# First layer of a graph network: who issues the edge-attribute loads

## The chip, the cores and the metric

The kernel runs on one core of a Trainium2 chip. The metric is the device time of one execution in microseconds (us); smaller is better. Before the change three runs gave 4244.64, 4257.71 and 4271.31 us, a median of 4257.71 us.

A core has five engines with an instruction stream each: TensorE (PE; its weight loads are PEld), VectorE (DVE), ScalarE (ACT), GpSimd (POOL) and SyncE (SP). SyncE computes nothing. DMA transfers are carried out by 16 DMA engines. An engine that issues a transfer spends an instruction on it; the transfer then runs by itself, and a semaphore tells of its landing. An engine executes its instructions in order: if one waits for a semaphore, all behind it wait too.

## The reference

Four layers are added to a residual stream `x` of 6250 nodes with 256 features; each begins with a layer norm. The change concerns the first one, a message-passing layer over 106,250 edges sorted by destination:

```
h   = relu(concat(xn[src], edge_attr) @ W1 + b1)     # one row per edge
agg = segment_sum(h, dst) / max(count, 1)            # mean over the edges of a node
x   = x + relu(concat(xn, agg) @ W2 + b2)
```

The attributes are 106,250 rows of 256 f32, about 109 MB, and each row is used once. The other three layers (graph attention with four experts, a second graph layer, and a mixture of small networks) are not touched.

## The kernel before

**Work of the first layer.** The product with W1 is split. `xn @ W1[:256] + b1` is computed once per node in an opening loop (L1534) and stored to a table in DRAM, `y_dram` (L1554, issued by SyncE). After that, each edge needs its attribute row times the other half of W1, plus the gathered row `y_dram[src]`.

Nodes are taken in 49 windows of 128. The edges of a window make a fixed stretch of tiles of 128 edges, cut into three groups of six tiles; so there are 147 groups, numbered `q`. For each group:

- `load_attr` (L1494) takes one of three `ea` buffers and lists the loads that fill it: the six tiles come in two or three runs of tiles that lie together, and each run is cut into four loads by column block (`for c in (0, 2, 1, 3)`). A group with three runs of two tiles has twelve loads of 64 KB, a group with two runs of three tiles has eight of 96 KB. Two groups of each window have three runs and one has two: 32 loads a window, 1568 in all.
- `issue` (L1515) starts the listed loads from the front of the list, each on the engine that its entry names.
- `turn` (L1610, `V.transpose` at L1613) transposes `ea` into `et` on VectorE. It is the only reader of `ea`, so its end frees the buffer.
- `hidden` (L1618) multiplies `et` with `w1b` on TensorE, two tiles at a call (the matmuls are recorded at L1170, in the helper `mm`).
- `load_sources` (L1603) gathers `y_dram[src]` by six indirect DMAs from GpSimd (L1184), into a ring of four buffers.
- `join` (L1628) adds both on VectorE (L1631) and takes the relu on ScalarE (L1632).
- `add_up` (L1635, L1650) sums the rows into their nodes on TensorE.

When a window's three groups are summed, `end_of` (L1656) finishes its nodes in small steps over the next groups: ScalarE scales and copies (L1663, L1165, L1685, L1691, L1702 to L1704), TensorE transposes (L1164) and multiplies (L1170), VectorE adds. Beside this, in the same loop, VectorE sorts the edges of the second layer, and `windows` prepares the edge indices of later windows (two small loads by SyncE for each window, L1202).

**Order.** The loop at L1741 writes the order out by hand, and `Ordered.pin` keeps it on every engine. In round `q` the loads for the next groups are handed out at three places (L1753, L1762, L1768), up to four from the list (`LOT = 4`) at each. Loads for group `q + 4` are listed after `turn(q + 1)`, whose end frees their buffer. In the opening loop, from the fifth block of nodes on, the loads of the first three groups are issued in one go (L1568, L1569), between the node work.

**Who issues.** The entry's engine is `SY if c < 2 or i == 2 else SC`. Of a group with three runs SyncE issues eight loads and ScalarE four, of a group with two runs each issues four; in total SyncE 980 and ScalarE 588. Each load's address depends on the window's first edge, a value that `start_of` (L1093) reads from SBUF into a register of both engines (TENSOR_LOAD at L1094).

**Semaphores of the loads.** In the trace the loads of both engines use eight semaphores in turn. A load waits until the load eight before it, whichever engine issued that one, has landed; the first load into a buffer also waits for VectorE's transpose.

Of the kernel before, what the change touches and what calls it, by code (L numbers as in the profile page):

```python
# [918 lines left out]
def kernel(ctx: ExitStack, tc: tile.TileContext, a: dict, out: bass.AP):  # L919
# [73 lines left out]
    V, SC, TE, GP, SY = nc.vector, nc.scalar, nc.tensor, nc.gpsimd, nc.sync  # L993
# [7 lines left out]
    with ExitStack() as fast:  # L1001
# [91 lines left out]
        def start_of(w, *also):  # L1093
            return nc.values_load(  # L1094
                start[0:1, w : w + 1], engines=(mybir.EngineType.SP, *also), min_val=0,
                max_val=E1 - WE, skip_runtime_bounds_check_because="it is clamped to that",
            )
# [350 lines left out]
        with ExitStack() as layer:  # L1448
# [45 lines left out]
            def load_attr(q):  # L1494

                w, g = groups1[q]
                parts = []
                ea = wea.tile([P, G1 * 4, 2 * Q], F32, name="ea")
                r = start_of(w, mybir.EngineType.Activation)
                rows = a["edge_attr_256"][bass.ds(r, WE), :]  # L1500
                at = 0
                for i, (first, n) in enumerate(RUNS[g]):
                    part = rows[first * P : (first + n) * P, :]
                    for c in (0, 2, 1, 3):
                        parts.append((
                            SY if c < 2 or i == 2 else SC,
                            ea[c * Q : (c + 1) * Q, at : at + 4 * n, :],
                            part[:, 2 * c * Q : 2 * (c + 1) * Q].rearrange(
                                "(m p) d -> p m d", p=Q
                            ),  # L1510
                        ))
                    at += 4 * n
                return ea, parts
# [8 lines left out]
            with (  # L1522
# [11 lines left out]
                for t0, t1 in parts0:  # L1534
# [32 lines left out]
                    if b >= 4:  # L1567
                        ahead[b - 4], parts = load_attr(b - 4)  # L1568
                        issue(parts, len(parts))  # L1569
# [3 lines left out]
            with (  # L1573
# [167 lines left out]
                for q in range(NQ1 + 2):  # L1741
                    if 0 < q <= NQ1:
                        join(q - 1)
                    if q < NQ1:
                        hidden(q, 0)
                    steps(keys or sort)
                    if q >= 2:
                        add_up(q - 2)
                        if (q - 2) % NG == NG - 1:
                            work.append(end_of((q - 2) // NG))  # L1750
                    if 3 <= q + 2 < NQ1:
                        load_sources(q + 2)
                    issue(parts, LOT)  # L1753
                    if q + 1 < NQ1:
                        turn(q + 1)
                    for n in range(q + 2, min(q + 5, NQ1)):
                        if n not in ahead:
                            ahead[n], more = load_attr(n)
                            parts += more
                    if q < NQ1:  # L1760
                        hidden(q, 2)
                    issue(parts, LOT)  # L1762
                    steps(keys or (sort if q % 4 else []))
                    if q < NQ1:
                        equals[q] = equal(wk, *groups1[q])
                        hidden(q, 4)
                    steps(slow)
                    issue(parts, LOT)  # L1768
                    ordered.pin()
# [1084 lines left out]
```

## Time and profile before

| | us |
|---|---|
| median of three runs | 4257.71 |
| the profiled execution, its own time | 4246.74 |
| its span on the core | 4244.9 |
| first layer's group loop, from about 100 to 1510 us of the span | 1410 |
| TensorE busy in that stretch | 1185.76 |
| VectorE, GpSimd, ScalarE busy in that stretch | 908.97, 854.48, 321.89 |

Some 2 us of the profiled execution lie outside its span. The page gives the busy time of each engine, the span in 40 slices, the DMA queues (q1 is filled by SyncE, q10 by ScalarE, q0 by GpSimd's gathers), and groups of instructions. Instructions that issue a DMA or wait for a semaphore are not counted as busy; they are marked with a q behind the engine (SPq, ACTq). The view of waits has one line for each pair of a waiting instruction and what ended its wait, with total, number of times and the longest; "issue" is idle time that ended with nothing that the profile shows, and "remote" is a semaphore whose sender it can't name.

### The profile page before, as it was taken

The page shows a single profiled execution, that of the slowest core. Times are in us where ns is not written, and L with a number is a line of the kernel's source. Part 1 is how long each engine was busy: PE and PEld are TensorE (multiplying, and loading weights), DVE is VectorE, ACT ScalarE, POOL GpSimd, SP SyncE. Part 2 cuts the span into 40 slices and gives each one's busy share as a digit, 9 for nine tenths or more (in the row PEclk, how much of TensorE's full clock was granted, in tenths as well). Part 3 has the DMA queues.
Part 4 walks back from the last instruction along what each step waited for, and adds up shares of the span by engine and source line. Part 5 has one row for each costly group of instructions (what it writes and reads, how often), then busy time and mean ns, then how long its engine had stood idle before and what let it go on. Part 6 is the DMA issues. An engine that isn't in the chain of part 4 may idle for free.

```text
span 4244.9 us, 59987 instructions
## 1 busy us (share of the span) xinstructions
PE 3208.8 (76%) x18517; PEld 2451.9 (58%) x18517; DVE 2192.9 (52%) x6516; ACT 1188.6 (28%) x2200; POOL 2256.7 (53%) x2720
## 2 busy tenths in 40 slices
PE   6788888888888767777787777794347777767787
PEld 5566666666666555566666665672235555555556
DVE  6666667665666535546464544674223333434344
ACT  4122222222222223334444443572002111111133
POOL 1655666566666543445454445424566666665551
PEclk8899999999999988889998988895567767667687
DMA  5666777667676632223232332343111111111110
GB/s 176 153 160 156 165 169 166 161 160 169 156 171 162 147 84 69 65 64 104 73 101 75 81 87 67 95 108 90 42 47 50 51 50 51 50 49 52 46 48 19
DMA packets 704935, 423.34 MB, mean 100 GB/s; under 512 B 538699, under 2 KB 647303, under 8 KB 704604
## 3 DMA queue, kind: packets, MB, share of 16 engines
q1 hardware_dynamic: 422972, 201.12, 17.9%
q0 software_dynamic: 88512, 171.58, 17.0%
q10 hardware_dynamic: 193120, 46.69, 5.1%
q8 instruction: 150, 2.46, 0.2%
q14 instruction: 181, 1.48, 0.1%
HBM read 382.75 MB, written 42.50 MB: 100 GB/s over the span
## 4 chain that ended last, share of the span: by engine, by line
PE 40%; another core or an unknown queue 18%; issue 9%; DVE 8%; ACT 3%; DMA 1%; SPq 1%; POOL 0%; ACTq 0%; DVEq 0%; POOLq 0%
PE ph L1170 17%; PE py L1170 10%; PE pe L2714 5%; PE pt L1170 3%; PE pe L1650 2%; PE po L2032 1%; DVE et L1613 1%; DVE E L2010 1%; DVE eq L2691 1%; PE pa L1955 1%; ACT L1833 1%; PE pt L1164 1%; DMA rb<-low_dram 0%; SPq L1518 0%
## 5 line engine op out<-in xcount | busy, mean ns | idle before, releaser
L1184 POOL DMA_INDIRECT h<-y_dram,src x882 | 857.3, 972 | 639.0 <-issue 336.6
L1184 POOL DMA_INDIRECT hg<-hp_dram,src x831 | 784.2, 944 | 486.3 <-issue 224.7
L1184 POOL DMA_INDIRECT sg<-gat_dram,src x612 | 595.3, 973 | 722.9 <-DVE pay L1992 312.2
L1170 PE MATMUL ph<-w1b,et 128*128 128x256 f32 x3528 | 882.5, 397 | 82.7 <-issue 67.2
L1170 PEld LDWEIGHTS ph<-w1b,et 128*128 128x128 f32 x3528 | 673.6, 197 | 273.2 <-issue 181.9
L1170 PE MATMUL py<-w,hh 128*128 128x256 f32 x1568 | 449.8, 425 | 107.6 <-issue 52.1
L2714 PEld LDWEIGHTS pe<-eq,hg 128*128 128x128 f32 x2036 | 380.0, 259 | 224.8 <-issue 161.6
L2714 PE MATMUL pe<-eq,hg 128*128 128x96 f32 (+15 forms) x2036 | 390.2, 339 | 122.2 <-issue 76.6
L1170 PE MATMUL ph<-b_all,w 128*128 128x256 f32 (+1 forms) x1600 | 460.3, 427 | 13.8 <-issue 12.5
L2691 DVE TENSOR_SCALAR eq<-px,dst,ew 128x96 f32<-128x96 f32 x831 | 262.0, 369 | 324.4 <-remote 148.3
L1631 DVE TENSOR_TENSOR h<-ph,h 128x1536 f32<-128x1536 f32 x147 | 258.1, 1756 | 323.0 <-PE pe L1650 109.8
L1170 PEld LDWEIGHTS py<-w,hh 128*128 128x128 f32 x1568 | 303.4, 208 | 170.8 <-issue 67.8
L1632 ACT ACTIVATE h<-h 128x1536 f32<-128x1536 f32 x147 | 218.3, 1485 | 587.6 <-DVE h L1631 176.9
L1170 PEld LDWEIGHTS ph<-b_all,w 128*128 128x128 f32 x1600 | 317.2, 214 | 59.4 <-issue 19.8
L2010 DVE TENSOR_SCALAR E<-nodes,bits 128x256 bf16<-128x256 bf16 (+5 forms) x612 | 187.0, 339 | 174.9 <-remote 78.3
L1613 DVE STREAM_TRANSPOSE et<-ea 128x1536 f32<-128x1536 f32 x147 | 260.7, 1774 | 14.6 <-issue 8.5
L1833 ACT ACTIVATE hh<-ph,b 128x256 f32<-128x256 f32 (+1 forms) x400 | 166.0, 465 | 293.4 <-remote 137.1
L1650 PE MATMUL pe<-h,eq 128*32 128x257 f32 x2496 | 202.6, 410 | 13.5 <-issue 12.0
L1170 PE MATMUL py<-ew,g 65*128 65x256 f32 x392 | 141.8, 491 | 63.7 <-DVE x_all L2667 20.0
L1833 ACT ACT_TABLE_LOAD x102 | 130.9, 1283 | 91.5 <-remote 51.4
L2667 DVE SCALAR_TENSOR_TENSOR x_all<-py,gate,x_all 128x256 f32<-128x256 f32 x196 | 93.9, 479 | 110.7 <-remote 68.0
L2032 PE MATMUL po<-pays,E 128*128 128x61 bf16 x2116 | 117.2, 198 | 41.7 <-issue 33.1
(358 smaller groups left out, 3947.5 us busy)
## 6 DMA issues: line engine op xcount, KB each, us to landing
ea<-in_edge_attr_dram SPq DMA_DIRECT2D x784, 64.0 KB
ea<-in_edge_attr_dram ACTq DMA_DIRECT2D x392, 64.0 KB
w<-in_L_ffn_W_dram SPq DMA_DIRECT2D x48, 512.0 KB
y<-ys SPq DMA_DIRECT2D x96, 256.0 KB
rb<-low_dram SPq DMA_DIRECT2D x84, 256.0 KB
ea<-in_edge_attr_dram ACTq DMA_DIRECT2D x196, 96.0 KB
ea<-in_edge_attr_dram SPq DMA_DIRECT2D x196, 96.0 KB
h<-y_dram,src POOLq DMA_INDIRECT x882
```

The costliest lines, as they stand in the source:

```text
L1170: TE.matmul(dst, lhs(c), rhs(c), start=c == 0, stop=c == n - 1)
L1184: GP.indirect_dma_start(out=dst, out_offset=None, in_=table[0:NP, :], in_offset=IndirectOffsetOnAxis(ap=idx, axis=0), **more,)
L1613: V.transpose(et[q].rearrange("p c m k -> p m c k"), ahead.pop(q).rearrange("p m (c k) -> p m c k", c=2),)
L1631: V.tensor_add(h, ph.pop(q), h)
L1632: SC.activation(h, h, AF.Relu)
L1650: TE.matmul(sums[w][b * Q : (b + 1) * Q, :], some[:, (b - lo) * Q : (b - lo + 1) * Q], rows_of(q)[:, j, 0:WS], start=(g, b, j) in begin, s ...
L1833: SC.activation(hidden[u][:, f, :n, :], ph[:, f - f0, :n, :], AF.Gelu, bias=b1[:, e, f : f + 1],)
L2010: V.tensor_scalar(Es[g, j][:, 0:n, :].rearrange("p b k -> p (b k)"), nodes16[:, 0 : n * P], bits.bitcast(F32)[:, g * G + j : g * G + j + 1 ...
L2032: TE.matmul(pos[g][bank][:, to * HP : (to + 1) * HP], E[:, b - b0, :], pays[g % 2][:, j, :], start=bank not in begun, stop=bank not in lat ...
L2667: V.scalar_tensor_tensor(x_all[:, t, :], py[:, k, :], gate[:, t, e : e + 1], x_all[:, t, :], op0=OP.mult, op1=OP.add,)
L2691: V.tensor_scalar(equals[k][:, j, :], lanes[:, 0:NW], dst_of[:, t : t + 1], ew[:, t : t + 1], op0=OP.is_equal, op1=OP.mult,)
L2714: TE.matmul(sums[b][:, lo - t0 * P : hi - t0 * P], hg[:, j, :], eq[:, j, lo - n0 : hi - n0], start=False, stop=after >= (t0 + n) * P,)
```

## The change

Every load of the attributes is issued by SyncE. The list, its order, the sizes, the lots of four, the three places in a round, the buffers and what they wait for are the same.

```diff
                     for c in (0, 2, 1, 3):
                         parts.append((
-                            SY if c < 2 or i == 2 else SC,
+                            SY,
                             ea[c * Q : (c + 1) * Q, at : at + 4 * n, :],
```

In the built program ScalarE has 588 loads fewer and SyncE 588 more. ScalarE's register reads at L1094 are gone as well, since nothing there uses them. In the group loop the order of instructions on VectorE and GpSimd is the same as before; TensorE differs only in how a few matmuls and transposes of the opening loop alternate.

## The prediction

> **What bounds the kernel now.** I read the busy table by stretches first, because the change touches only the group loop, then the waits of TensorE, ScalarE and SyncE in its steady part, 200 to 1400 us, and last single moments. The table by stretches (columns after the length: PE, PEld, DVE, ACT, POOL busy, TensorE clock, DMA share, GB/s):
>
> ```profile
> core 0: us, PE busy (x) PEld busy (x) DVE busy (x) ACT busy (x) POOL busy (x), PEclk, DMA share, GB/s
> 200.00:1400.00 1200.00, 1015.16 (x5844) 744.37 (x5846) 786.70 (x1612) 277.75 (x460) 729.52 (x751) 0.95 0.69 162
> ```
>
> TensorE is busy 85% and nobody else over 66%: it is the bound, with 185 us of idle time in 1200. 124.5 groups pass in that time (147 in 1410 us), 9.6 us each. So the question is what the change does to TensorE's idle time. The waits of TensorE in the same window:
>
> ```profile
> PE ph L1170 <- issue: 60.1, 105, 1.7
> PE pt L1164 <- ACT a_dst L1704: 43.2, 13, 8.1
> PE pt L1170 <- issue: 21.6, 27, 4.8
> PE pt L1164 <- ACT o L1691: 20.9, 2, 13.0
> PE ph L1170 <- DVE et L1613: 5.8, 6, 2.0
> ```
>
> TensorE hardly ever waits for attributes (the transpose `et`: 5.8 us), and never for the relu. It waits for ScalarE in the steps of `end_of`, and for "issue". Of the two waits for `o` the longer is this moment, first on TensorE, then on ScalarE:
>
> ```profile
> 217.11 0.69 PE L1164 MATMUL pt<-ident,o 128*128 128x128 f32 x2 [13.03 <-ACT o L1691]
> ...
> 199.69 0.18 ACT L1685 ACTIVATE ln_rs<-ln_rs 128x1 f32<-128x1 f32 x1
> 214.81 1.52 ACTq L1518 DMA_DIRECT2D ea<-in_edge_attr_dram  x2
> 216.46 0.60 ACT L1691 ACTIVATE o<-x_all,off,ln_rs 128x256 f32<-128x256 f32 x1 [16.58 <-DMA ea<-in_edge_attr_dram]
> ```
>
> ScalarE stands from 199.9 to 214.8 before a load: its semaphore is still held by loads that SyncE issued, and the activation that TensorE needs is queued behind it. The views of ScalarE's and SyncE's waits, same window:
>
> ```profile
> ACT h L1632 <- DMA ea<-in_edge_attr_dram: 102.8, 23, 11.5
> ACT o L1691 <- DMA ea<-in_edge_attr_dram: 41.2, 3, 16.6
> ACT o L1663 <- DMA ea<-in_edge_attr_dram: 18.1, 5, 5.6
> ...
> SPq L1518 <- DVE et L1613: 120.3, 25, 12.1
> ```
>
> ScalarE spends 162 us on such waits beside the issuing itself. SyncE waits for a free buffer: it is ahead of the need.
>
> **What SyncE gives and takes.** SyncE's queue at two moments, eight loads in clean passage and four beside two of ScalarE's:
>
> ```profile
> 1124.27 5.06 SPq L1518 DMA_DIRECT2D ea<-in_edge_attr_dram  x8
> ...
> 1130.20 3.98 SPq L1518 DMA_DIRECT2D ea<-in_edge_attr_dram  x4
> ```
>
> 0.63 us a load against 1.00. In the second case register moves of 29 ns take 664 and 700 ns each. From the single records of SyncE, 200 to 1400 us, end of one issue to end of the next: 713 loads that aren't the first of their buffer take 0.875 us on average. The 521 of them that have packets of ScalarE's queue in the microsecond before or during them take 0.977, the other 192 take 0.596. 125 first loads take 481 us, 316 of it waiting for the transpose and 165 issuing with their register read; 83 index loads take 85. Sum 624 + 481 + 85 = 1190 of 1200 us.
>
> **A reason for the difference**, from the DMA queues between 600 and 1000 us (packets, MB, share of 16 engines):
>
> ```profile
> q0 software_dynamic: 11953, 31.03, 29.5%
> q1 hardware_dynamic: 83917, 20.46, 23.5%
> q10 hardware_dynamic: 54688, 13.03, 15.4%
> ```
>
> A packet of q10 takes 0.154 x 16 x 400 us / 54688 = 18 ns, so the engines pass at most 16 / 0.018 = 889 a microsecond, some 627 beside the gathers. A load of 64 KB is 256 packets; at 0.52 us a load (the median of the 192) one issuer makes 492 a microsecond, two make 984. One stays below 627, two do not. That this back-pressure is what stops the sequencers is an estimate of mine; that they are slower while both queues run is measured. It isn't certain at every moment: in the clean stretch above ScalarE also issued four loads.
>
> **The change part by part.**
>
> *ScalarE loses 588 issues.* In 200 to 1400 us these are 500 at a median of 0.33 us for the DMA instruction alone, about 0.5 with moves, 250 us in all, and 162 us of waits. Nearly all of it lies beside TensorE's work: relu has a whole round to spare. On the path are the steps of `end_of` that TensorE waits for because ScalarE stood before a load: the two `o` waits, 20.9 us, or 25 over 1410 us. Next late there is VectorE's `off`, done at 200.3 us in the moment above: TensorE's own matmuls, which end at 204.1, come after it, so the whole wait goes.
>
> *SyncE gains 588 issues.* In the 1200 us: 1213 x 0.596 = 723, plus 165 and 85, makes 973 us, 81%. So it stays ahead, and its waits for the buffer shrink from 316 us to some 200. The last load of a group is issued 8 or 12 x 0.6 = 5 to 7 us after its buffer is free and has landed 2 to 3 us later (median landing of SyncE's loads 1.6 to 2.1 us); it is wanted three rounds, 28 us, after that. Hidden by that lead, cost 0. What it costs without that cover is rival C. The index loads (L1202) queue behind more loads, but are asked for a block of seven windows ahead.
>
> *The semaphores.* Eight in turn, now all SyncE's: 8 x 0.6 = 4.8 us pass until one comes round, against a landing of 2 to 3 us. No new wait.
>
> *Slow sequencers go.* This the trace can't show; I bound it. The share of SyncE's loads over 1 us is 40% with ScalarE's packets and 9% without. TensorE's idle share is 15.1% overall and 8.2% where no sequencer instruction of SyncE or ScalarE took 0.6 to 0.76 us in the 8 us before. The most that can go is the difference, 6.9% of 1200 = 82 us, the parked `o` waits among it. Three quarters of it, as 40% falls to 9%, is 62, and 62 x 1410/1200 = 72 us. The least is the 25 us above: a correlation need not be a cause. A loss from this part is excluded only if SyncE keeps ahead. I take 60, nearer to 72, since the slow instructions are measured on the very queue that is changed.
>
> *The opening loop loses.* 26 loads instead of 18 stand on SyncE ahead of the last stores of `y_dram`, for which the gathers wait: 8 x 0.52 = 4 us. ScalarE's first four issues took 3.3 us between its activations (70.1 to 73.4 us), and those go. Between 0 and 4; I take +3.
>
> **A rule against it.** The Trainium skill, "DMA: Bandwidth & Descriptors", section "Issuing engines are not separate DMA queues", says that several issuing engines share the same 16 DMA engines, so issuing from more of them saves only the sequencer's own time. By that rule there is nothing to gain from one queue, and ScalarE's share of the issuing time was saved for nothing lost: the gain would be the 25 us alone, less 3, so -22. The rows say that the second queue isn't free, 0.977 against 0.596 us. I go by the rows.
>
> **Sum.** -60 + 3 = -57 us on the profiled execution: 4246.7 - 57 = 4190. The median of the runs lies 11 us above that execution, so 4257.7 - 57 = 4201 us.
>
> **The rivals.**
>
> *B, ScalarE is freed, the stalls stay:* only -25 + 3 = -22, so 4236. For it: TensorE's "issue" waits are short, 105 of them with 1.7 us at most, and could be its own. Against it: stalls of TensorE, SyncE and ScalarE come in the same microseconds.
>
> *C, SyncE becomes the bound:* if a load keeps costing 0.875 us when all come from one queue, SyncE needs 1213 x 0.875 + 250 = 1311 us where there are 1200: the loop grows by 9.3%, 130 us, and VectorE's transpose waits for attributes; 4257.7 + 130 = 4388. It decides from (1200 - 250) / 1213 = 0.78 us a load on; at 0.977 it would be +280. For it: the slowness needs GpSimd's gathers too, and they stay. Against it: 0.596 without ScalarE's packets, 177 of these 192 beside gathers.
>
> *D, TensorE's clock takes it back:* the granted clock falls as TensorE idles less, and the time is as before, about 4255. Against it: 0.95 in this stretch, and it fell to half just in the idle stretches that begin at 1135, 1335 and 1392 us.
>
> That the change doesn't do what it says is excluded: the built program has no load of the attributes on ScalarE.
>
> **How the numbers follow.** This kernel's runs spread by 0.6% about their median; about 1% is what a measurement can tell from no change. Forecast A (4201, by its bounds 4170 to 4236): 0.48. B (4236): 0.20. C (4300 to 4540, 4388 at the rate above): 0.20. D (4255): 0.12. Faster by over 1% is below 4215: four fifths of A, a fifth of B, some of still larger gains: 0.45. Slower by over 1% is above 4300: C, 0.20. Within: 0.35. The range holds A, B and D, and of C the mild part: 4150 to 4340. Since TensorE's work alone is 1185.76 us in 1410, more than 220 us can't go.
>
> **What would show it.** No ACTq load; relu and `o` no longer waiting for `ea`; SyncE's mean below 0.7 us a load with few instructions of 700 ns; TensorE busy 88 to 89% of the loop, which ends near 1455; all after it unchanged. Wrong would be: VectorE's L1613 waiting tens of microseconds for `ea` (C), TensorE's idle share still 15% with no slow instructions (B), or a clock below 0.93 (D).

## The result, and the profile after

The change made the kernel slower. Five runs of each gave a median of 4317.95 us (4310.16 to 4324.09) against 4262.12 us before (4244.64 to 4293.87). The medians differ by 56 us, 1.3%; the ratio on record is 1.0155, 95% interval 1.0124 to 1.0186. The forecast was 4201 us, a gain. The time lies inside the stated range (4150 to 4340), but in the part of it that belonged to rival C.

The profiled execution after took 4310.16 us. Its span is 4308.2 us, 63.3 us more than the one of before. By the first and the last transpose of `ea` (L1613) the group loop went from 101.4 to 1512.6 us before, and goes from 104.8 to 1560.7 now. So the opening loop lost 3.4 us, the group loop 44.7, and what is left, 15 us, lies in later stages that the change doesn't touch (2732 and 2748 us). Four traces of one other chip, shown below, differ there by 30 us (2688 to 2718), so I read nothing into it.

The table by stretches of the changed kernel, with the columns of the prediction's first fence:

```profile
200.00:1400.00 1200.00, 991.64 (x5674) 735.59 (x5672) 764.16 (x1576) 269.74 (x444) 701.95 (x724) 0.93 0.64 156
```

TensorE does less in the same 1200 us, and so does everybody else; no engine became busier. Over the whole loop TensorE's idle time rose from 222.8 to 258.6 us, 36 of the 44.7. The other 9 are longer busy time, at a granted clock of 0.92 instead of 0.94. The waits, same window (waiting instruction, what ended its wait: total us, times, longest):

```profile
DVE et L1613 <- DMA ea<-in_edge_attr_dram: 207.2, 63, 16.7
...
PE ph L1170 <- DVE et L1613: 54.2, 12, 13.1
...
PE pt L1164 <- ACT a_dst L1704: 29.0, 8, 6.1
```

Before, the first of these lines was

```profile
DVE et L1613 <- DMA ea<-in_edge_attr_dram: 3.0, 12, 0.6
```

VectorE's transposes now wait for attributes, 207 us against 3.0, and behind them TensorE waits 54.2 us where it waited 5.8. The two `o` waits of TensorE are gone, as forecast. The longest line in the view of SyncE's own waits in that window is now

```profile
SPq L1518 <- DMA ea<-in_edge_attr_dram: 7.5, 11, 1.4
```

The line of before, 120.3 us of waiting for the transpose to free a buffer, is missing: SyncE never comes early any more. All lines of this view together come to 14 us of waiting, against 194 in the same view of before. So SyncE has hardly a pause left.

Its single records, counted as in the prediction, say what it issues. 1165 loads that aren't the first of their buffer take 0.806 us each, 939 us; 120 first loads take 174 (before: 481); 84 index loads 87. That these add up to the 1200 us proves nothing: each is counted from the end of one issue to the end of the next, waits included, and before they added up to 1190. The proof is that the waits in them are gone.

One moment shows what that does. These are rows of the timeline (start, length, instruction, idle time before it and its releaser; SPq is SyncE issuing):

```profile
784.96 6.72 SPq L1518 DMA_DIRECT2D ea<-in_edge_attr_dram  x7
...
792.63 0.01 SPq L1202 DMA_DIRECT2D raw_src<-in_src_dram  x1
...
806.25 0.28 SPq L1202 DMA_DIRECT2D raw_dst<-in_dst_dram  x1
807.13 24.72 SPq L1518 DMA_DIRECT2D ea<-in_edge_attr_dram  x39
812.84 1.78 DVE L1613 STREAM_TRANSPOSE et<-ea 128x1536 f32<-128x1536 f32 x1 [16.73 <-DMA ea<-in_edge_attr_dram]
...
814.67 3.78 PE L1170 MATMUL ph<-w1b,et 128*128 128x256 f32 x8 [12.52 <-DVE et L1613]
```

From 791.7 to 807.1 SyncE issues fourteen index loads, and no attribute load. VectorE then stands 16.7 us, TensorE 12.5. There are six such blocks in the loop; beside them lie five of the long waits of the transpose (16.16, 15.30, 11.05, 16.73 and 8.69 us). Before the change SyncE issued the same blocks, and no transpose waited for them: it came early then.

### The profile page after: what moved, and what is told of

Same layout as the page of the kernel before. It is cut to its first block, busy times and chain, and to the rows that moved or that the text cites. A ratio compares the mean times of both kernels' runs of the same rounds, so it can differ in the third digit from the quotient of the medians.

```text
span 4308.2 us, 59824 instructions
## 1 busy us (share of the span) xinstructions
PE 3228.7 (75%) x18517; PEld 2469.9 (57%) x18517; DVE 2188.7 (51%) x6516; ACT 1187.9 (28%) x2200; POOL 2254.6 (52%) x2720
## 4 chain that ended last, share of the span: by engine, by line
PE 31%; another core or an unknown queue 17%; issue 6%; DVE 6%; ACT 3%; DMA 1%; SPq 1%; POOL 0%; DVEq 0%; ACTq 0%
PE ph L1170 11%; PE py L1170 10%; PE pe L2714 4%; PE pt L1170 2%; PE po L2032 1%; DVE eq L2691 1%; PE pa L1955 1%; SPq L1518 1%; DVE E L2010 1%; ACT L1833 1%; ACT hh L1833 1%; DVE x_all L2667 1%; PE py L2264 0%; DVE ys L1849 0%
## 5 line engine op out<-in xcount | busy, mean ns | idle before, releaser
L1613 DVE STREAM_TRANSPOSE et<-ea 128x1536 f32<-128x1536 f32 x147 | 261.1, 1776 | 321.8 <-DMA ea<-in_edge_attr_dram 276.7
L2032 PEld LDWEIGHTS <-E 128*128 128x128 bf16 x2116 | 103.9, 102 | 84.0 <-issue 62.2
```

The source lines that it names most:

```text
L1613: V.transpose(et[q].rearrange("p c m k -> p m c k"), ahead.pop(q).rearrange("p m (c k) -> p m c k", c=2),)
L2032: TE.matmul(pos[g][bank][:, to * HP : (to + 1) * HP], E[:, b - b0, :], pays[g % 2][:, j, :], start=bank not in begun, stop=bank not in lat ...
```

## The experiments

Two things must be known first. The experiments fell on five chips. The kernel before takes 4191 and 4194 us on two of them and 3299 to 3303 us on the other three. So every time is compared on its own chip, and the kind is named: chips of 4200 us and chips of 3300 us. For the pair of the result no chip is on record. Its 4262 us lies above every run of before on the other two chips of 4200 us (4216.4 at most), and its later stages are the longest in both traces, so I take it to be a third chip of that kind, the same for both kernels.

And the prediction's "slow sequencers" can be counted: SyncE's register moves before its loads in the loop that take 600 to 760 ns instead of some 30 to 50, called slow moves from here on. The pair of the result has 201 of 1918 before and 286 of 3078 after. The chips of 3300 us have none.

My theory after the result was this: SyncE's rate sets the loop, at 0.8 us a load, and nothing that ScalarE was freed of is worth anything. Its rivals: any load moved from ScalarE to SyncE costs in proportion; the loss lies in the order of the loads; the loss belongs to that one chip.

**How many loads SyncE can take.** Two other shares, on a chip where the kernel before takes 4194.22 us. SyncE gets 1274 of the 1568 loads:

```diff
-                            SY if c < 2 or i == 2 else SC,
+                            SC if c == 3 and i < 2 else SY,
```

> ScalarE issues only the column block c = 3 of a group's first two runs, SyncE the rest: 1274 and 294 loads in place of 980 and 588 (before) or 1568 and 0 (all on SyncE). Theory S (SyncE's throughput is the bound once it has all loads: 0.81 us a load whoever else issues): SyncE needs 1043 x 0.81 + 250 = 1095 of 1200 us, so it keeps just ahead; VectorE's transposes wait less than 60 us for attributes, and with ScalarE parked half as often the time is that of before or a little less, 4235 to 4270 us. Rival L (each load moved to SyncE costs the same, 56 us for 588): half of the loss, near 4290 us.

Measured: 4193.31 us, ratio 0.9989 (0.996 to 1.0017). SyncE's waits in 200 to 1400 us and what is left of the transposes' wait, in the views of waits of this kernel:

```profile
SPq L1518 <- DVE et L1613: 77.5, 21, 6.7
...
DVE et L1613 <- DMA ea<-in_edge_attr_dram: 2.1, 8, 0.6
```

SyncE still comes early, VectorE waits for nothing, and nothing is lost, although a load costs 0.853 us here, more than in the changed kernel. A cost in proportion would be half of the loss, some 0.6 to 0.8%, and the interval shuts that out: half of the move (294 of 588) costs nothing on this chip. The whole move wasn't run on it. The other way, each engine 784:

```diff
-                            SY if c < 2 or i == 2 else SC,
+                            SY if c < 2 else SC,
```

> SyncE and ScalarE issue half each, 784 and 784 loads (of every group the blocks c = 0, 1 by SyncE). Theory S: SyncE is less loaded than before but wasn't the bound there, so nothing is won on its side, and ScalarE issues 196 loads more and is parked longer: 4265 to 4310 us, TensorE waiting longer for ScalarE in the steps of end_of. Rival L: 19 us less than before, near 4243 us.

Measured: 4201.66 us, ratio 0.9975 (0.9942 to 1.0007), no difference that the runs can show. ScalarE waits 182 us for `ea` here (162 in the profile before), with no effect on the time.

**Whether ScalarE's waits cost anything.** The kernel before with ScalarE's loads at the end of each group's list:

```diff
-                return ea, parts
+                return ea, sorted(parts, key=lambda v: v[0] is SC)
```

> The split of before, but in each group's list the loads of SyncE stand ahead of those of ScalarE, so that ScalarE's come at a later place of the round, when the buffer is free. If ScalarE's being parked before loads costs TensorE time (my 25 us from the two long waits), the waits of o and h for attribute loads shrink from 162 us to under 80 and the time falls by 10 to 30 us, to 4230 to 4250. If parking costs nothing on the path, the same as before within 0.5%.

Measured: 4195.58 us, ratio 0.9993 (0.9961 to 1.0024). The edit missed its aim, as the views of waits of this kernel show, of the engines first and then of SyncE's queue:

```profile
ACT o L1691 <- DMA ea<-in_edge_attr_dram: 94.3, 32, 9.5
ACT o L1663 <- DMA ea<-in_edge_attr_dram: 74.6, 24, 11.1
ACT h L1632 <- DMA ea<-in_edge_attr_dram: 59.3, 18, 16.7
...
SPq L1518 <- DMA ea<-in_edge_attr_dram: 181.1, 45, 9.3
```

ScalarE's waits rose to 228 us, and SyncE stands 181 us behind semaphores of earlier loads. But that is information too. The waits before the two activations of `end_of` are 169 us here against 59 in the profile before, and the time stayed where it was.

**All on SyncE, but fewer loads.** From the fourth group on, the third run of a group isn't loaded (the buffer's old content is used in its place, so that part of the attributes is left out); three named buffers in turn stand for those of the pool (what they do by themselves wasn't tested), and SyncE issues all loads:

```diff
-                for i, (first, n) in enumerate(RUNS[g]):
+                for i, (first, n) in enumerate(RUNS[g] if q < 3 else RUNS[g][:2]):
...
-                            SY if c < 2 or i == 2 else SC,
+                            SY,
```

> All loads on SyncE, but from the fourth group on the third run of a group is not loaded (stale attributes stand in its place), and the three buffers are named ones used in turn: about 980 loads on SyncE, as many as before, none on ScalarE, a quarter of the bytes gone. Theory S: SyncE is ahead again, VectorE's transposes wait under 30 us for attributes in place of 277, and the group loop ends some 50 to 100 us sooner than with all loads, near or under the time of before (4170 to 4260). If SyncE's throughput is not what costs the time, it stays near 4318.

Measured: one run of 4203.13 us. The loop takes 1411.6 us; in the three kernels above, on the same chip, it takes 1397.2, 1404.3 and 1402.3. Of its views of waits, those of TensorE, VectorE and SyncE, 200 to 1400 us:

```profile
PE pt L1164 <- ACT a_dst L1704: 63.2, 11, 9.5
...
DVE et L1613 <- DMA ea<-in_edge_attr_dram: 23.0, 10, 11.3
...
SPq L1518 <- DVE et L1613: 69.7, 17, 8.3
...
SPq L1202 <- DMA gat_dram<-gtab: 19.0, 1, 19.0
```

With some 290 loads fewer in these 1200 us (991 against 1285), at 0.873 us each, SyncE has pauses again, and the transposes' wait falls from 207 to 23 us. Two waits, 9.9 and 11.3 us, make up nearly all of the 23. Ahead of each SyncE stood some 20 us inside a block of index loads, the second time behind a store of ScalarE (`gtab` to `gat_dram`, the last line above). So what was lost to SyncE's rate is gone here. The kernel with all 1568 loads wasn't run on this chip.

The hoped-for gain isn't there even so: ScalarE is as free as in the changed kernel, and TensorE idles 213 us in the loop, as in the other three (213, 206, 213). The two long waits of the transposes cost TensorE 9.6 us of that, so a gain of some 10 us could hide behind them. The waits for `o` are gone, 20.9 us in the profile before, but those for `a_dst` are 63.2 us instead of 43.2. That one took the place of the other is likely but not shown: the two profiles are of two chips, and with each engine issuing 784 loads TensorE waited 30.4 us for `a_dst` and none for `o`.

**The changed kernel again.** I wanted the loss on a second chip, with two edits that take away what might slow a load: five of a group's six gathers (their rows of the buffer keep what the groups before left there, so the gathered part is left out), and half of each load's rows (the other half of the attributes is left out).

```diff
-                    for j, t in enumerate(tiles_of[g]):
+                    for j, t in enumerate(tiles_of[g][:1]):
```

```diff
-                            ea[c * Q : (c + 1) * Q, at : at + 4 * n, :],
-                            part[:, 2 * c * Q : 2 * (c + 1) * Q].rearrange(
+                            ea[c * Q : (c + 1) * Q, at : at + k * n, :],
+                            part[0 : k * n * Q, 2 * c * Q : 2 * (c + 1) * Q].rearrange(
```

Here `k` is 2 instead of 4 from the fourth group on, and the buffers are named as above.

> The changed kernel again, on the chip of the other runs, as the mark for them. Theory S: the same loss as measured first, 45 to 65 us over before, SyncE without a pause in the group loop and VectorE's transposes waiting 200 to 300 us for attributes.

> All loads on SyncE, but of a group's six gathers only the first is issued (the other five tiles keep stale rows). If GpSimd's gathers beside the loads make SyncE slow, a load falls from 0.81 us to under 0.62, the share over 1 us from 27% to under 8%, and VectorE's transposes no longer wait for attributes (under 40 us in place of 277). If SyncE is slow of its own packets or of its instructions, it stays near 0.8 and the transposes still wait.

> The kernel before with the same gathers left out. If gathers are the cause, SyncE's loads fall under 0.65 us here too, also beside packets of ScalarE's queue (0.977 with all gathers), and this kernel and the one with all loads on SyncE differ by less than 15 us in the group loop. If the two load queues disturb each other, the loads beside ScalarE's packets stay over 0.85 us.

> All loads on SyncE, all 1568 and all gathers, but from the fourth group on each load brings only the first half of its rows (stale attributes for the rest; three named buffers): half the packets at the same number of instructions. If the back-pressure of the loads' own packets slows SyncE (my estimate of 492 packets a microsecond against 627), a load falls under 0.65 us and the loop under 1420 us. If the packets of the loads don't matter, a load stays at 0.75 to 0.85 us and the loop near 1455.

Measured, on a chip where the kernel before takes 3298.58 us: the changed kernel 3307.1, ratio 1.0028 (1.0017 to 1.0039); with few gathers 3282.53; the kernel before with few gathers 3267.82; with half rows 3286.25 (one run each of these three). The expected 45 to 65 us are missed widely, because the slow moves aren't there: none of 3078 is over 0.06 us, and a load costs 0.584 us. The table by stretches and SyncE's waits of the changed kernel on this chip, 200 to 1100 us:

```profile
200.00:1100.00 900.00, 867.24 (x5408) 676.36 (x5409) 729.57 (x1501) 253.08 (x423) 674.93 (x692) 0.98 0.90 199
```

```profile
SPq L1518 <- DMA gat_dram<-gtab: 41.2, 3, 16.2
SPq L1202 <- DMA gat_dram<-gtab: 28.2, 2, 14.7
SPq L1518 <- DVE et L1613: 27.7, 22, 3.3
```

TensorE is busy 96%, a group takes 7.8 us instead of 9.9. SyncE has pauses, but stands five times some 14 us before a load whose semaphore is still held by a store of ScalarE: `gtab` to `gat_dram`, seven windows at a time (L1705 to L1708). That is a new suspect for the small loss on the chips of 3300 us. So I took the changed kernel with one store of all 49 windows at the end in place of seven:

```diff
-                    if w % TB == TB - 1:
+                    if w == T - 1:
                         yield
-                        sl = slice(w - TB + 1, w + 1)
+                        sl = slice(0, T)
```

> The changed kernel on one more chip, since on the last one both kernels took 3300 us and no register move of SyncE took over 0.2 us. If what makes the change cost time is the slow sequencer (register moves of 0.6 to 0.76 us), then on a chip whose trace shows such moves (some 10% of them) the loss is 40 to 65 us, and on one whose trace shows none it is 5 to 15 us.

> All loads on SyncE, and ScalarE's seven stores of gat_dram (one for every seven windows, L1708) become one store of all windows when the last one is done. On the last chip SyncE stood up to 16 us before a load whose semaphore was held by such a store (57 us in 4 waits). If that is what is left of the loss on a chip without slow moves, this kernel there takes the time of before within 0.2% (loss under 5 us), and no SyncE load waits for gat_dram. On a chip with slow moves it changes little (under 15 us), since SyncE has no pause there anyway.

> All loads on SyncE, only the first gather of six in each group (stale rows in the other five tiles). On a chip with slow moves: if the gathers are needed for them, their share falls from 10% to under 3% and a load from 0.81 us to under 0.62; if not, a load stays near 0.8. On a chip without slow moves the load stays at 0.55 to 0.6 us, as on the last one.

> All loads on SyncE and all gathers, half the rows of each load from the fourth group on (stale attributes for the rest, three named buffers). On a chip with slow moves: if the packets of the loads themselves make them (back-pressure), a load falls under 0.65 us and the loop by some 40 us; if not, a load stays at 0.75 to 0.85 us. On a chip without slow moves 0.58 us, as on the last one.

This was a chip of the same kind (before: 3302.55 us), so the loss I looked for was again not there. The changed kernel took 3307.59, ratio 1.0017 (1.0007 to 1.0027); few gathers 3278.39, half rows 3295.68, one run each. With one store it took 3291.74 (3285.67 to 3298.15), ratio to before 0.9966 (0.9952 to 0.998). Its view of SyncE's waits, 200 to 1100 us, begins with

```profile
SPq L1518 <- DVE et L1613: 62.5, 28, 4.9
```

and has no line for `gat_dram`. The waits of the transposes for `ea` in this window fell from 49.4 us (the changed kernel on the same chip) to 9.0.

**What makes SyncE slow.** These three ran on a chip of 4200 us (before: 4191.18 us).

> All loads on SyncE, only the first gather of six in each group (stale rows in the other five tiles). On a chip with slow moves: if the gathers are needed for them, their share of the register moves falls from 10% to under 3% and a load from 0.81 us to under 0.62; if not, a load stays near 0.8. On a chip without: 0.55 to 0.6 us.

> All loads on SyncE and all gathers, half the rows of each load from the fourth group on (stale attributes for the rest, three named buffers). On a chip with slow moves: if the loads' own packets make them (back-pressure), a load falls under 0.65 us and the loop by some 40 us; if not, a load stays at 0.75 to 0.85. On a chip without: 0.58 us.

> The kernel before with ScalarE's seven stores of gat_dram made one. If the edit only takes away SyncE's waits that the change had brought (SyncE runs far ahead only when it has all loads), the time is that of before within 0.2%. If the stores cost time by themselves, it gains as much as the one-store version with all loads on SyncE, 0.3% to 0.6%.

The changed kernel with a sixth of the gathers took 3905.5 us in its one run, 286 less than the kernel before. The table by stretches:

```profile
200.00:1100.00 900.00, 879.12 (x5508) 688.47 (x5507) 736.66 (x1523) 258.83 (x435) 112.34 (x117) 0.99 0.52 122
```

Its loop takes 1114.2 us, as with the same few gathers on the chips of 3300 us (1117.0 and 1114.9), a load 0.568 us, and no register move of SyncE takes 600 ns. So on these chips the slow moves come with GpSimd's gathers: on one and the same chip they are there with all gathers, in the two kernels that follow, and gone with a sixth. The second queue isn't needed for them, for the changed kernel has none for the attributes and 286 slow moves. The later stages, which keep all their gathers, take 2688 us here as in the other traces from chips of 4200 us.

Half rows took 4221.07 us in one run. There are 237 slow moves among 3078 and a load costs 0.763 us. Its table by stretches, and what its transposes wait for in 200 to 1400 us:

```profile
200.00:1100.00 900.00, 765.85 (x4365) 564.07 (x4364) 603.28 (x1263) 208.03 (x343) 536.53 (x554) 0.94 0.46 119
```

```profile
DVE et L1613 <- DMA ea<-in_edge_attr_dram: 86.5, 38, 11.5
```

Again SyncE has hardly a pause (its view lists 26 us of waits in these 1200, 0.3 of it for a transpose), and the loop takes 1417.0 us against 1398.8 in the next kernel on this chip. So the packets of the loads themselves are not what slows it. Nor is it the amount of traffic: this kernel moves 119 GB/s at a DMA share of 0.46, the one with few gathers 122 at 0.52. Whether the gathers' packets do it or GpSimd's issuing of them, no run separates. The kernel before with one store took 4190.97 us, ratio 0.9994 (0.996 to 1.0029); it has 181 slow moves among 1918.

Two more counts from these traces. The slow moves are a mark of it, not the whole: of the gaps between a register move and the DMA instruction behind it 105 of 1040 last 0.55 to 0.76 us in the changed kernel's first trace, and 8 of 1308 on a chip of 3300 us (200 to 1100 us). And ScalarE hardly has them. Of its own register moves before loads none of 1176 is slow in the trace of before, where SyncE has a tenth; with 784 loads on each engine it is 38 of 1568 against 183. So the change gave loads from an engine that issues them smoothly to the one that stutters. Why the two differ, no run shows.

**A fourth trial of the changed kernel**, and the one store in both kernels on one chip.

> The changed kernel again. Theory (SyncE's rate is the bound where a load costs about 0.8 us): if register moves of 600 to 760 ns are there, a load that isn't the first of its buffer costs 0.79 to 0.83 us, SyncE makes no pause, VectorE's transposes wait 170 us or more for attributes, and the kernel is 40 to 60 us over the one before. If those moves are absent, the load costs 0.57 to 0.59 us and the kernel is 4 to 9 us over the one before. Rival (the loss of the first comparison belonged to that chip): within 15 us of the one before although the slow moves are there.

> The changed kernel with one store of ScalarE for the attention layer's edges instead of seven. Theory: where slow moves are there, SyncE has no pause to lose, so the store's semaphore matters little and it stays within 15 us of the changed kernel; where they are absent, it is 12 to 18 us below the changed kernel, as once before. Rival (the store's semaphore is a good part of the loss everywhere): 25 us or more below the changed kernel with slow moves there.

> The kernel before with one store instead of seven. Where slow moves are there: within 5 us of the one before, as measured once. Where they are absent: if the gain of the changed kernel with one store belongs to the store alone, 8 to 15 us under the one before; if it needs SyncE as the only issuer, within 4 us of it.

This was a chip of 3300 us (before: 3299.82). The changed kernel took 3309.02, ratio 1.0028 (1.0017 to 1.0038); with one store 3296.37, 0.9989 (0.9979 to 0.9998); the kernel before with one store 3300.83, 1.0 (0.999 to 1.0009). So the one store by itself is worth nothing in the kernel before, and 13 to 16 us in the changed one. On the chips of 3300 us that takes back the whole loss and leaves the pair 0.1 to 0.3% under the kernel before. Whether it helps the changed kernel on a chip with slow moves wasn't measured. SyncE waited 0.2 us for these stores there, having no pause to lose, so I would expect little.

## Why the prediction was wrong

**The step that failed: "SyncE gains 588 issues" at 0.596 us, cost 0.** The load costs 0.806 us when all come from one queue, so 1213 loads need 978 us and not 723. With 250 us of the rest SyncE needs 1228 us of 1200, and the lead that was to hide everything is used up. Rival C gave the threshold, 0.78 us, and named the victim, VectorE's transpose; both held. So did its argument that the slowness needs the gathers, which stay. The half rows, at 0.763 us, lie just at the point, with hardly a pause left and a smaller loss. C's size was off because it took 0.875 us: at 0.806 its formula gives 2.3% of the loop, some 33 us. The rest of the measured 44.7 I can't split further. One part of it C left out: its 85 us of index loads are no even stream, they come in six blocks of 12 to 16 us.

**Why 0.596 was wrong.** It was the mean of those loads near which ScalarE's queue had no packets, 192 of 713. I read it as the effect of ScalarE's queue; it was mostly a selection. With that queue gone, 1159 of the 1165 loads have no such packets near them, and take 0.802 us. The mean of all loads fell from 0.875 to 0.806 us only.

Part of the error is in how the class was made: "in the microsecond before or during" the load. A load that lasts long has a longer time in which to meet a packet, so slow loads fall into the class with packets because they are slow. Asked only for the microsecond before the load begins, the same trace of before gives 278 loads without a packet of that queue, at 0.732 us, and 435 with one, at 0.966. With 0.732 SyncE would have needed 1138 us of 1200, 95% and not 81%, before its index blocks are thought of. Asked in this way for gathers, the trace after gives 303 loads without at 0.581 and 862 with at 0.885. I had noted that 177 of the 192 lay beside gathers and took it as evidence against C, but the 192 had in part been picked for being short.

**"Slow sequencers go", -60.** They stay: 286 of 3078 moves after, 201 of 1918 before, 9% and 10%. So the 82 us of TensorE's idle time (6.9% of 1200) that I tied to them didn't go with the second queue; the idle time grew. That the gathers bring them, on some chips only, is shown by the run with a sixth of them. My estimate of packets that back up in the engines fails with it: with half the packets a load still cost 0.763 us, with few gathers 0.568, on the same chip.

**"ScalarE loses 588 issues", -25.** The two `o` waits went, as said, but no gain of 25 us with them. The run with fewer loads has ScalarE as free and SyncE with pauses, and TensorE idles as in the three kernels with ScalarE's loads on the same chip. A wait that is long on a list of waits wasn't a gain to be had. Likely the next step of the same chain, ScalarE's copies (`a_dst`), comes late in its place; I had looked only at `off` as what comes next, and in one moment. Rival B rests on the same 25 us and fails with it. Rival D, the clock, had no trial, since TensorE idled more and not less.

**The rule.** The Trainium skill, "DMA: Bandwidth & Descriptors", section "Issuing engines are not separate DMA queues", says that a second issuing engine saves just the sequencer's own time. I used it for a milder gain, -22 us. Read the other way it spoke of the loss: the sequencer's time was the thing that ran short, with 14 us of waits left to SyncE in 1200.

**What was right.** ScalarE waits for no load any more: relu and `o` no longer stand before `ea`. The semaphores brought no new wait among the loads (7.5 us, 13.2 before). With ScalarE's stores, which I hadn't looked at, they did wherever SyncE had pauses: on the chips of 3300 us and in the run with fewer loads. The opening loop lost 3.4 us for the +3 forecast, but that is little of a test: on the chips of 3300 us the three traces of the changed kernel reach the group loop at 99.6, 100.7 and 101.9 us.

**What stays open.** The loss of 56 us itself was measured once, in the first pair. On the two other chips with slow moves I ran variants of the changed kernel, which behave as the theory says, but not that kernel. So that SyncE's rate is the cause rests on the trace of that pair and on these variants. Another order of the loads on SyncE's one queue wasn't tried. Why some chips have the slow moves and others don't, no run shows.

## What to carry to other kernels

Before all loads are given to one queue, add up that queue's whole round (loads, register reads, and whatever comes in blocks) with the mean cost of a load over all moments, and never with that of a chosen part. A class made by what happens during an instruction picks out the long ones; make it by what happens before. Look for slack in the waits, not in a sum from end to end, which always fills the window. An engine that issues transfers needs slack for the longest block that it issues in one go, here 15 us. A wait on the list is a gain only if the chain behind it has nothing else that comes late by as much.

## What the runs showed of the hardware

The kernel before takes 4191 to 4262 us on some chips and 3299 to 3303 on three others, 21 to 23% less. In the loop of the changed kernel the difference is 1455.9 against 1144.2 us. Most of it is idle time of TensorE, 258.6 against 49 us. On the chips of 4200 us about a tenth of SyncE's register moves take 600 to 760 ns, and hardly any of ScalarE's (0 of 1176 in the trace of before); on the chips of 3300 us none of SyncE's is over 51 ns in the trace of the changed kernel, with the same program and the same gathers. On a chip of 4200 us they vanish too when five of six gathers are left out, and the loop is then as long as with few gathers on a chip of 3300 us, 1114 us against 1115 and 1117.

On the chips of 3300 us a load costs 0.51 us in the median, 64 or 96 KB or half of that. On the others the median is nearly the same, 0.52 us in the changed kernel; it is the mean that differs, 0.806 against 0.584.

In each trace of the changed kernel on a chip of 3300 us, stores by ScalarE held up SyncE's loads six times, 12 to 16 us each, through a semaphore that both use in turn. Making one store of the seven removed these waits and 13 to 16 us of the time.
